# Seven half-size products in place of eight for the q and k of six sequences, in an attention and feed-forward kernel

## The chip, the cores and the metric

The kernel runs on one core of one Trainium2 chip. The metric is the device time of one execution in microseconds (us). The engines are PE (TensorE, matrix products), DVE (VectorE), ACT (ScalarE), POOL (GpSimd) and SP, whose instructions here are DMA issues. Each engine works its own instructions in order, and waits for others by semaphores.

## What is computed

Eight sequences of 512 rows and 256 columns are normalised and go through two branches whose outputs are multiplied: a causal attention with a window of 250 positions, 16 heads of 16 columns and rotated q and k ("rope"), and a three-layer feed-forward part whose weights are +1 or -1.

```python
xn = _layernorm(x)
proj = xn @ in_proj_w.T                      # 256 -> 3 * 256: q, k, v
q, k = _apply_rope(q, k)                     # ya = xa*cos - xb*sin, yb = xa*sin + xb*cos
mask = (delta >= 0) & (delta < CONTEXT)      # delta = row - column, CONTEXT = 250
scores = where(mask, q @ k.T * D ** -0.5, lowest)
s = (softmax(scores) @ v) @ out_proj_w.T
h = s0 * conn_dense(k0, concatenate([xn, -xn])); h = relu(h) * 2
h = s1 * conn_dense(k1, h);                      h = relu(h) * 2
g = silu(s2 * conn_dense(k2, h))
x = x + s * g
```

## The kernel before

**Layout.** Everything is held transposed: 128 partitions carry columns (or heads), the free axis the 512 positions T of a sequence. The 256 columns of q are sorted so that part "a" (128) holds the first member of each rotated pair and part "b" the second; the same for k.

**Order.** Instructions are issued from a list of pieces, each with a time written by hand, in units of which a sequence takes 42 (`SEQ`); a piece can return further pieces with delays, which `run` (L234) keeps in a heap and issues when the running cost has passed their time. The order in which they are issued is the order on every engine. While sequence b goes through its 16 feed-forward layers' tiles and its 6 attention steps, the inputs of sequence b + 1 are prepared: in units of b, its moments at 9, normalisation at 18.4, k at 23.0 and 24.5, q at 26.0 and 27.5.

**Normalisation.** `norm_turned` (L300) subtracts and multiplies the transposed x (`xT`) by the moments spread over partitions (`of_all`, L309, on DVE), and splits the result into a 16-bit high part (ACT) and a low part (DVE) for the feed-forward layers. `of_all` has one buffer (tag "mb", shared with part b of the rope products).

**Feed-forward.** `layer` (L511 products, L520 low part `h2l` on DVE, L522 high part `h2h` on ACT) is what PE does most of the time. Products of high parts ("h high") and of low parts ("h low") of a tile can be issued apart. `z` is the last layer (L562), whose silu needs an exponential, a sum, a reciprocal (L633, DVE, in halves) and a product with the gate (L635, POOL).

**q and k.** `project` (L371) makes 128 columns by 512 positions in one PSUM bank from two products (L381: two chunks of 128 columns of x). Each product is one instruction in the program and two records in the profile. DVE multiplies the bank by cosine and sine (`rope_sb`, L397: two operations of 128x512, reading PSUM), POOL adds and subtracts the four (`rotate`, L418), ACT rounds the result into a high half (`split_hi`, L434, tag "hi": one buffer for k and q), DVE makes the low half as the difference (`split_lo`, L441), and each half is written to DRAM at once by two DMAs of 512 KB on SP (`to_dram`, L427: `dk`, `dq`). `stack` (L450) loads them back, 16 partition rows of several heads at a time, as the operands of the scores (`k<-dk`, `q<-dq`, 256 KB each).

**Attention.** A step is six banks of scores (`sc`, L746), exponentials (L771, ACT), masks of the window (L791, L798, POOL) and products with v (`po`, L828) of the step before. `keep` (L840) moves a group's result to `V` and its row sums to `S` (three buffers; L846 and L847 on DVE, L852 and L853 on ACT); `gather` (L918, `dsums<-S`), `pack` (L926, `sums<-dsums`), `invert` (L932 to L938) and `unpack` (L945) turn the sums into reciprocals via DRAM, and `divide` spreads them (`R`, L951) and multiplies `V` (L952, POOL). `project_o` (`att_ps`, L962) and L984, L991 finish the output with the residual `xr` (loaded by L545). The last sequence has outputs of 256 positions, with a copy of PSUM on ACT (L974) and sums on POOL (L975, L977).

PSUM has eight banks: seven rotate over all uses that ask for `bank(...)`, one is kept for `po`.

Of the kernel before, what the change touches and what calls it, by code (L numbers as in the profile page):

```python
# [11 lines left out]
F32 = mybir.dt.float32  # L12
# [22 lines left out]
def tile_attention_times_gated_ffn(  # L35
# [62 lines left out]
    work = ctx.enter_context(tc.tile_pool(name="work", bufs=2))  # L98
    small = ctx.enter_context(tc.tile_pool(name="small", bufs=4))
    hpool = ctx.enter_context(tc.tile_pool(name="hpool", bufs=1))  # L100
    probs = ctx.enter_context(tc.tile_pool(name="probs", bufs=8))
    dram = ctx.enter_context(tc.tile_pool(name="dram", bufs=2, space=bass.MemoryType.DRAM))
    PSUM = bass.MemoryType.PSUM
    ps_o = ctx.enter_context(tc.tile_pool(name="ps_o", bufs=1, space=PSUM))
# [2 lines left out]
    def bank(name):  # L107
        return ps_b.tile([P, T], F32, tag="b", name=name)
# [56 lines left out]
    def weights(w, p, c, cols):  # L165
        if p == "l":
            return w[:, c, cols]
        return w[:, c].bitcast(F16).rearrange("p (f two) -> p f two", two=2)[:, cols, 1]

    rows = const.tile([P, T], F32, name="rows")  # L170
    nc.vector.memset(rows, 1.0)
# [119 lines left out]
    def lay_over(b):  # L291

        st = states[b]
        of_all = st["of_all"] = turned.tile(
            [P, 2, T], F32, tag="mb", name=f"of_all_{b}", bufs=1
        )
        d = st["moments"].rearrange("(i t) p -> i (t p)", i=2)
        nc.sync.dma_start(of_all, d.partition_broadcast(P))

    def norm_turned(b, c):  # L300

        st = states[b]
        if c == 0:
            st["xT"] = raw_xT.pop(b)
            for p, dt in (("h", F16), ("l", F32R)):
                st["x" + p] = one.tile([P, EC, T], dt, tag="x" + p, name=f"x{p}_{b}")
        xT = st["xT"][:, c]
        for i, op in ((1, ALU.subtract), (0, ALU.mult)):
            nc.vector.tensor_tensor(xT, xT, st["of_all"][:, i], op)  # L309
        hi, lo = (st["x" + p][:, c] for p in "hl")  # L310

        def low():
            nc.vector.scalar_tensor_tensor(lo, xT, sgnx, hi, ALU.mult, ALU.subtract)

        return [(3.2, lambda: nc.scalar.mul(hi, xT, sgnx)), (3.8, low)]

    def norm(b, t):
        mv, xn = states[b]["mv"], xs[b, t]
# [52 lines left out]
    def project(b, what, part, half=None):  # L371

        st = states[b]
        col = E * "qk".index(what) + P * "ab".index(part)
        if half == 1:
            ps = st.pop(part)
        else:
            ps = st[part] = bank(f"{what}{part}_ps_{b}")
        for cols in [slice(0, T)] if half is None else [ts(half, T // 2)]:
            for c in range(EC):  # L380
                nc.tensor.matmul(  # L381
                    ps[:, cols], wqkv_sb[:, c, ds(col, P)], st["xT"][:, c, cols],
                    start=(c == 0), stop=(c == EC - 1),
                )
        if half == 0:
            return

        m = turned.tile(
            [P, 2, T], F32, tag=f"m{part}", name=f"m_{what}{part}_{b}",
            bufs=2 if part == "a" else 1,  # L390
        )
        st[what, part] = m

        hi_after, lo_after = (4.0, 5.1) if b else (5.0, 6.2) if what == "k" else (4.6, 5.4)

        def times(i):
            nc.vector.tensor_tensor(  # L397
                m[:, i], ps, rope_sb[:, i if part == "a" else 1 - i], ALU.mult
            )

        def both():
            times(0)
            times(1)
            if part == "b":
                return [
                    (1.4, lambda: rotate(b, what)),
                    (hi_after, lambda: split_hi(b, what)),
                    (lo_after, lambda: split_lo(b, what)),
                ]


        return [(1.5 if b == 0 and what + part == "qb" else 0.0, both)]

    def rotate(b, what):
        st = states[b]
        m, n = st[what, "a"], st.pop((what, "b"))
        for i, op in enumerate((ALU.subtract, ALU.add)):
            nc.gpsimd.tensor_tensor(m[:, i], m[:, i], n[:, i], op)  # L418
# [34 lines left out]
    def prepare(b, plain=False):  # L453

        if b == 0 or plain:
            at = dict(stats=-40, norm=-38, x=-36, k=0, q=3, v=9.2)
            dp, dv = 1.5, 1.5
        else:

            at = dict(load=9, stats=9, down=10.5, over=12, norm=18.4, k=23.0, q=26.0, v=SEQ + 0.6)  # L460
            if b == 1:
                at.update(load=17.15, stats=14, down=16.9, over=17.2, norm=24.8, k=28.1, q=31.6)
            dp, dv = (0.01 if b == 1 else 1.5), 0.85
            at = {n: SEQ * (b - 1) + f for n, f in at.items()}
        out = [(at["stats"], 0, lambda: stats(b))]
        if "over" in at:
            out += [
                (at["load"], 0, lambda: load_xT(b)), (at["down"], 0, lambda: lay_down(b)),
                (at["over"], 0, lambda: lay_over(b)),
                (at["norm"], 0, lambda: norm_turned(b, 0)),  # L470
                (at["norm"] + 1.2, 0, lambda: norm_turned(b, 1)),
            ]
        for t in range(NT):
            if "over" not in at:
                out += [
                    (at["norm"] + t, 0, lambda t=t: norm(b, t)),
                    (at["x"] + t, 0.25, lambda t=t: turn_x(b, t, plain)),
                ]
            out.append((at["v"] + dv * t, 0.87, lambda t=t: project_v(b, t)))
        for what in "kq":  # L480
            for n, part in enumerate("ab"):
                if b == 0 and what == "k" and not plain:

                    out += [
                        (-34.3 if n == 0 else -32.95, 0.87, lambda p=part: project(b, "k", p, 0)),
                        (at["k"] + dp * n, 0.87, lambda p=part: project(b, "k", p, 1)),
                    ]
                else:
                    out.append((
                        at[what] + dp * n, 1.75, lambda w=what, p=part: project(b, w, p),  # L490
                    ))
        return out
# [37 lines left out]
    def beside(b, u, tag):  # L530

        st = states[b]
        if b + 1 == B and u % 2:
            return st[tag][:, T // 2 :]
        if b + 1 == B and u == 2 and tag == "xr":

            st[tag] = turned.tile([P, 2, T], F32, tag="mb", name=f"xr_{b}_{u}", bufs=1)[:, 0]
        else:
            st[tag] = work.tile([P, T], F32, tag=tag, name=f"{tag}_{b}_{u}", bufs=1)
        return st[tag][:, : T // 2] if b + 1 == B else st[tag]  # L540

    def residual(b, u):
# [296 lines left out]
    def keep(b, g, po):  # L839

        st = states[b]
        odd = g % 2
        S = st["S", g] = outs.tile([P, T], F32, tag="S", name=f"S_{b}_{g}", bufs=3)
        if odd:
            V = st["V", g // 2]
            nc.vector.scalar_tensor_tensor(V, po, second_half, V, ALU.mult, ALU.add)  # L846
            nc.vector.tensor_copy(S, po)  # L847
        else:
            V = st["V", g // 2] = outs.tile(
                [P, T], F32, tag=f"V{g // 2}", name=f"V_{b}_{g}", bufs=2  # L850
            )
            nc.scalar.mul(V, po, first_half)  # L852
            nc.scalar.copy(S, po)  # L853

# [92 lines left out]
    def divide(b, pair):  # L947
        st = states[b]
        V = st["V", pair]
        R = outs.tile([P, T], F32, tag="S", name=f"R_{b}_{pair}", bufs=3)  # L950
        nc.vector.stream_shuffle(R, rows, [D * (n // D) for n in range(32)])  # L951
        return [(0.5, lambda: nc.gpsimd.tensor_tensor(V, V, R, ALU.mult))]  # L952

# [51 lines left out]
    def divisions(b, pairs=(0, 1)):  # L1005
        out = []
        for pair in pairs:
            if b + 1 < B:
                first = SEQ * b + (30.0 if b else 38.4) if pair == 0 else SEQ * (b + 1) + 3.0
            else:  # L1010
                first = SEQ * b + (22.5 if pair == 0 else 33.4)
            pieces = (gather, pack, invert, unpack, divide)
            very_last = b + 1 == B and pair == 1
            for f, at in zip(
                pieces,
                (0.0, 2.0, 4.4, 6.4, 9.0) if very_last
                else (0.0, 2.4, 5.2, 7.6, 15.0 if pair and b + 2 < B else 10.6),
            ):
                out.append((first + at, 0, lambda p=pair, f=f: f(b, p)))
        return out  # L1020
# [17 lines left out]
    def swap():  # L1038
# [5 lines left out]
        (-34.6, 0, signs), (-40.5, 0, lambda: warm(9)), (-34.7, 0, lambda: warm(0)),  # L1044
        (-31.0, 0, lambda: enough(0)),
        (-32.7, 0, lambda: first_parts(2, 3)),
        (19.2, 0, make_w2), (22.5, 0, swap), (SEQ * (B - 1) + 47.6, 0, add_up),
        (SEQ * (B - 1) + 44.0, 0, hint),
    ]
    for c in range(EC):  # L1050
# [153 lines left out]
```

## Time and profile before

Three runs took 599.13, 599.91 and 601.34 us (median 599.91). The profiled execution took 598.2 us, of which 596.5 lie between its first and last instruction; the TensorE clock granted was 0.999 of full speed.

| what | us |
|---|---|
| median of the runs | 599.91 |
| profiled execution | 598.2 |
| its span | 596.5 |
| one sequence in the steady part | 72.05 |
| PE busy in each of the stretches 96:168, 168:240, 240:312, 312:384 | 72.00 |
| DVE, ACT, POOL busy there, mean of one stretch | 41.23, 36.43, 32.82 |
| one product of 128x512 for k or q (2 records) | 0.86 |
| rope multiply, one of 128x512 (L397) | 0.68 |
| low half of q, L441, mean of 8 | 2.09 |
| low half of k, L441, mean of 8 | 1.25 |
| reciprocal of 128x256, mean of 28 | 1.74 |

How to read the views: a timeline row has start and duration in us, engine, line, operation, the tile written, the tiles read, the shapes and a count of instructions; in brackets stand the idle time before it and what ended it. A row of the chain of waits has start, duration, engine, tile, line and count. In the table of stretches the four busy times stand in order PE, PEld (weight loads), DVE, ACT, POOL, with the number of instructions in brackets.

### The profile page before, as it was taken

What the parts mean: (1) busy time and instruction counts of PE and PEld (TensorE: products, weight loads), DVE (VectorE), ACT (ScalarE), POOL (GpSimd) and SP (SyncE); (2) the same over time, 40 slices, a digit from 0 to 9 for tenths busy, and PEclk for the clock granted to TensorE, in tenths of its full rate; (3) what the DMA queues carried; (4) which work ended last, traced back from release to release, by engine and by line L of the source; (5) the groups of instructions that cost most, each with busy time, mean ns of one, the idle gap of its engine ahead of it and who ended that gap; (6) DMA issues with size and microseconds to landing.
All of it is one profiled execution on the core that took longest, in us unless ns stands there. A gap on an engine that the chain in (4) does not pass through costs nothing.

```text
span 596.5 us, 10410 instructions
## 1 busy us (share of the span) xinstructions
PE 584.8 (98%) x3788; PEld 364.7 (61%) x3788; DVE 333.7 (56%) x578; ACT 303.0 (51%) x571; POOL 269.9 (45%) x474
## 2 busy tenths in 40 slices
PE   7999999999999999999999999999999999999996
PEld 6655565655655556555566556665566555657785
DVE  6936335666346754478436684366744666427256
ACT  4747564545464545536454465544644645465422
POOL 2736533436334552445444355333652437435513
PEclk9999999999999999999999999999999999999999
DMA  9764844337432474415654075441673335441111
GB/s 277 283 234 143 294 152 127 108 141 250 146 117 98 170 240 133 147 65 223 208 165 154 2 293 189 130 142 65 238 228 113 107 135 208 158 143 43 35 28 53
DMA packets 50086, 92.24 MB, mean 155 GB/s; under 512 B 10992, under 2 KB 18672, under 8 KB 50032
## 3 DMA queue, kind: packets, MB, share of 16 engines
q1 hardware_dynamic: 47600, 89.31, 44.1%
q10 hardware_dynamic: 2432, 2.23, 1.2%
q8 instruction: 31, 0.51, 0.3%
q14 instruction: 23, 0.19, 0.1%
HBM read 53.22 MB, written 38.30 MB: 153 GB/s over the span
## 4 chain that ended last, share of the span: by engine, by line
PE 88%; DVE 3%; DMA 3%; ACT 2%; SPq 1%; POOL 1%; issue 1%; DVEq 0%; POOLq 0%; ACTq 0%
PE h_ps L511 44%; PE po L828 11%; PE z_ps L562 9%; PE sc L746 7%; PE v_ps L361 4%; PE att_ps L962 4%; PE ka_ps L381 2%; PE qb_ps L381 2%; PE qa_ps L381 2%; PE kb_ps L381 2%; DMA of_all<-d 1%; DMA dq<-m_qa 1%; PE warm L232 1%; SPq L450 1%; DMA dk<-kh 1%
## 5 line engine op out<-in xcount | busy, mean ns | idle before, releaser
L771 ACT ACTIVATE p<-sc 128x512 f32<-128x512 f32 (+2 forms) x288 | 150.2, 607 | 57.6 <-PE sc L746 57.4
L791 POOL TENSOR_SCALAR_AFFINE_SELECT p<-p 128x256 f32<-128x256 f32 (+1 forms) x224 | 104.8, 479 | 123.1 <-ACT p L771 105.4
L511 PE MATMUL h_ps<-h1l,w_sb 128*128 128x512 f32 (+1 forms) x576 | 145.3, 394 | 0.0
L511 PE MATMUL h_ps<-h1h,w_sb 128*128 128x512 f16 (+1 forms) x576 | 123.1, 356 | 0.0
L511 PEld LDWEIGHTS h_ps<-h1l,w_sb 128*128 128x128 f32 x576 | 100.4, 188 | 27.4 <-issue 5.7
L511 PEld LDWEIGHTS <-w_sb 128*128 128x128 f16 x704 | 61.3, 98 | 86.3 <-issue 41.5
L522 ACT ACTIVATE h2h<-h_ps 128x512 f16<-128x512 f32 (+1 forms) x72 | 39.6, 550 | 133.1 <-PE h_ps L511 133.1
L520 DVE SCALAR_TENSOR_TENSOR h2l<-h_ps,h2h 128x512 fp32r<-128x512 f32 (+1 forms) x72 | 44.8, 622 | 93.9 <-ACT h2h L522 93.4
L828 PE MATMUL po<-p,v_pad 128*32 128x378 f32 (+4 forms) x1152 | 71.5, 380 | 0.0
L520 DVE SCALAR_TENSOR_TENSOR h1l<-h_ps,h1h 128x512 fp32r<-128x512 f32 x64 | 43.2, 688 | 45.3 <-ACT h1h L522 45.1
L798 POOL TENSOR_SCALAR_AFFINE_SELECT p<-p 128x256 f32<-128x256 f32 x144 | 57.5, 399 | 0.3 <-POOL p L791 0.3
L746 PEld LDWEIGHTS sc<-q,k 64*128 64x128 f32 x576 | 41.9, 186 | 25.0 <-issue 15.1
L633 DVE RECIPROCAL den<-den 128x256 f32<-128x256 f32 (+1 forms) x32 | 52.4, 1641 | 3.7 <-ACT den L628 3.7
L746 PE MATMUL sc<-q,k 64*128 64x378 f32 (+4 forms) x576 | 52.2, 310 | 2.2 <-ACT p L771 1.2
L522 ACT ACTIVATE h1h<-h_ps 128x512 f16<-128x512 f32 x64 | 37.6, 603 | 30.0 <-PE h_ps L511 30.0
L511 PE MATMUL h_ps<-xl,w_sb 128*128 128x512 f32 x128 | 52.3, 489 | 0.0
L952 POOL TENSOR_TENSOR V<-V,R 128x512 f32<-128x512 f32 x16 | 21.2, 1327 | 52.4 <-DVE R L951 52.4
L828 PEld LDWEIGHTS po<-p,v_pad 128*32 128x32 f32 x1152 | 30.7, 109 | 21.2 <-issue 12.0
L991 POOL TENSOR_TENSOR gate<-gate,xr 128x512 f32<-128x512 f32 (+1 forms) x15 | 18.6, 1242 | 47.6 <-DVE gate L984 26.6
L418 POOL TENSOR_TENSOR m_qa<-m_qa,m_qb 128x512 f32<-128x512 f32 x16 | 21.1, 1343 | 38.5 <-DVE m_qb L397 38.5
L511 PE MATMUL h_ps<-xh,w_sb 128*128 128x512 f16 x128 | 38.5, 383 | 0.0
L562 PE MATMUL z_ps<-h2l,w_sb 128*128 128x512 f32 (+1 forms) x144 | 35.6, 389 | 0.0
(102 smaller groups left out, 656.9 us busy)
## 6 DMA issues: line engine op xcount, KB each, us to landing
k<-dk SPq DMA_DIRECT2D x64, 256.0 KB
q<-dq SPq DMA_DIRECT2D x64, 256.0 KB
dk<-kh SPq DMA_DIRECT2D x16, 512.0 KB
dk<-m_ka SPq DMA_DIRECT2D x16, 512.0 KB
dq<-qh SPq DMA_DIRECT2D x16, 512.0 KB
dq<-m_qa SPq DMA_DIRECT2D x16, 512.0 KB
x<-in_x_dram SPq DMA_DIRECT2D x30, 128.0 KB
xT<-in_x_t_dram SPq DMA_DIRECT2D x7, 512.0 KB
```

What stands on the lines that cost most here:

```text
L361: nc.tensor.matmul(v.rearrange("p n s d -> p (n s d)"), st["xT"][:, c, ts(t, P)], wqkv_sb[:, c, 2 * E :], start=(c == 0), stop=(c == EC - 1),)
L381: nc.tensor.matmul(ps[:, cols], wqkv_sb[:, c, ds(col, P)], st["xT"][:, c, cols], start=(c == 0), stop=(c == EC - 1),)
L511: nc.tensor.matmul(ph, weights(w, p, c, ts(f, P)), st[src + p][:, c, cols], start=(k == 0), stop=(k == n - 1),)
L520: nc.vector.scalar_tensor_tensor(lo, ph, 0.0, hi, ALU.max, ALU.subtract)
L522: high = lambda: nc.scalar.activation(hi, ph, AF.Relu)
L562: nc.tensor.matmul(pz, weights(w2, p, c, ts(f, P)), st["h2" + p][:, c, cols], start=(c == 0 and p == "h"), stop=(c == NF1 - 1 and p == "l"),)
L633: nc.vector.reciprocal(part, part)
L746: nc.tensor.matmul(sc[r + (4 if y else 2 * pair)][:, ds(at, n)], st["k", g, pair][row, ts(j, P)], st["q", g, pair][row, ds(j * P + first, n)],
L771: nc.scalar.activation(p, s_, AF.Exp, scale=D ** -0.5)
L791: nc.gpsimd.affine_select(out=block, in_=block, compare_op=ALU.is_ge, fill=0.0, base=0, pattern=[[0, heads], [1, P]], channel_multiplier=-1,)
L798: nc.gpsimd.affine_select(out=block, in_=block, compare_op=ALU.is_ge, fill=0.0, base=-1, pattern=[[0, heads], [-1, beyond]], channel_multi ...
L828: nc.tensor.matmul(po[32 * r : 32 * r + 32, ds(j * P + first, n)], v_columns(j, g, r), place(tiles_, r, y, off, n), start=(j == 0), stop=( ...
```

## The change

For sequences three to eight (b from 2 to 7), q and k are made by another scheme. A projection of 256 columns into 2 x 128 of q (or k), over 512 positions, is read as a product of a 2 x 2 block matrix of weights with a 2 x 2 block matrix of x (chunks of 128 columns by halves of 256 positions): eight products of 128x128 by 128x256. The new code makes it from seven, with four sums of weight blocks (`w_sums`, made once on POOL for k and q together) and four sums of x blocks (`sum_x`, POOL, 128x256, after `norm_turned` of each chunk, in the buffer of tag "hi").

`project_seven` issues them in two phases into two banks: four products in phase 0, one for each half of each bank; then ACT copies the left half of each bank into SBUF and DVE adds the right half (`u`, and `y` in the tile of part b); three products in phase 1 add to what the banks hold (the left half of both banks and the right half of the second one). Then `quarters` make the four results in SBUF: one copy on ACT, three adds on DVE. The rope multiplies are eight operations of 128x512 in total for k and q, as before, but read SBUF and write in place. `rotate`, `split_hi` and `split_lo` are unchanged; their delays are longer. The pieces stand at 23.0, 24.7, 24.71 and 26.4 units in place of 23.0, 24.5, 26.0 and 27.5.

To make room: `probs` has 7 buffers in place of 8, `S` two in place of three, `R` takes the buffer of tag "hi", `den` moves to the pool `outs`, and the tiles of tag "mb" have two buffers. The last piece of `divisions` for the second pair stands at 14.0 in place of 15.0. Sequences one and two are projected as before.

```diff
-    probs = ctx.enter_context(tc.tile_pool(name="probs", bufs=8))
+    probs = ctx.enter_context(tc.tile_pool(name="probs", bufs=7))
...
+    w_sums = const.tile([P, 4, 2, P], F32, name="w_sums")
+
+    def of_w(c, half):
+        return wqkv_sb[:, c, : 2 * E].rearrange("p (w a f) -> p w a f", w=2, a=2)[:, :, half]
+
+    def sum_weights():
+        s1, s2, s3, s4 = (w_sums[:, i] for i in range(4))
+        sub = lambda out, a, b: nc.gpsimd.tensor_tensor(out, a, b, ALU.subtract)
+        nc.gpsimd.tensor_tensor(s1, of_w(0, 1), of_w(1, 1), ALU.add)
+        sub(s2, s1, of_w(0, 0))
+        sub(s3, of_w(0, 0), of_w(0, 1))
+        sub(s4, of_w(1, 0), s2)
...
         of_all = st["of_all"] = turned.tile(
-            [P, 2, T], F32, tag="mb", name=f"of_all_{b}", bufs=1
+            [P, 2, T], F32, tag="mb", name=f"of_all_{b}", bufs=2
...
+        if b > 1:
+            sum_x(b, c)
...
+    def sum_x(b, c):
+
+        st = states[b]
+        if c == 0:
+            st["x sums"] = turned.tile([P, 4, T // 2], F32, tag="hi", name=f"xs_{b}")
+        t1, t2, t3, t4 = (st["x sums"][:, i] for i in range(4))
+        x11, x12 = (st["xT"][:, 0, ts(k, T // 2)] for k in range(2))
+        x21, x22 = (st["xT"][:, 1, ts(k, T // 2)] for k in range(2))
+        sub = lambda out, a, b: nc.gpsimd.tensor_tensor(out, a, b, ALU.subtract)
+        if c == 0:
+            sub(t1, x12, x11)
+        else:
+            sub(t2, x22, t1)
+            sub(t4, x21, t2)
+            sub(t3, x22, x12)
...
-            bufs=2 if part == "a" else 1,
+            bufs=2,
...
+    def project_seven(b, what, phase):
+
+        st = states[b]
+        H2 = T // 2
+        n = "kq".index(what)
+        w = "qk".index(what)
+        s1, s2, s3, s4 = (w_sums[:, i, w] for i in range(4))
+        w11, w12, w22 = (of_w(c, half)[:, w] for c, half in ((0, 0), (1, 0), (1, 1)))
+        t1, t2, t3, t4 = (st["x sums"][:, i] for i in range(4))
+        x11, x21, x22 = (
+            st["xT"][:, c, ts(half, H2)] for c, half in ((0, 0), (1, 0), (1, 1))
+        )
+
+        def products(which, start):
+            for bank_, half, a, b_ in which:
+                nc.tensor.matmul(
+                    st["seven"][bank_][:, ts(half, H2)], a, b_,
+                    start=start and half == 0, stop=True, skip_group_check=True,
+                )
+
+        if phase == 0:
+            st["seven"] = [bank(f"{what}{i}_ps_{b}") for i in range(2)]
+            products(((0, 0, w11, x11), (0, 1, s2, t2), (1, 0, s3, t3), (1, 1, s1, t1)), True)
+            u = st["u"] = outs.tile([P, H2], F32, tag="u", name=f"u_{what}_{b}")
+            first, second = st["seven"]
+            for part in "ab":
+                st[what, part] = turned.tile(
+                    [P, 2, T], F32, tag=f"m{part}", name=f"m_{what}{part}_{b}", bufs=2
+                )
+            y = st[what, "b"][:, 1, H2:]
+
+            def sums():
+                for out, ps in ((u, first), (y, second)):
+                    nc.scalar.copy(out, ps[:, :H2])
+                    nc.vector.tensor_tensor(out, out, ps[:, H2:], ALU.add)
+
+            return [(0.0, sums)]
+
+        products(((0, 0, w12, x21), (1, 0, w22, t4), (1, 1, s4, x22)), False)
+        first, second = st["seven"]
+        u, m, o = st["u"], st[what, "a"], st[what, "b"]
+
+        def quarters():
+            nc.scalar.copy(m[:, 1, :H2], first[:, :H2])
+            nc.vector.tensor_tensor(m[:, 1, H2:], second[:, H2:], u, ALU.add)
+            nc.vector.tensor_tensor(o[:, 1, :H2], second[:, :H2], u, ALU.add)
+            nc.vector.tensor_tensor(o[:, 1, H2:], o[:, 1, H2:], u, ALU.add)
+            return [(0.3 if n else 2.0, times)]
+
+        def times():
+            for t, order in ((m, (0, 1)), (o, (1, 0))):
+                for i, r in enumerate(order):
+                    nc.vector.tensor_tensor(t[:, i], t[:, 1], rope_sb[:, r], ALU.mult)
+            hi_after = 6.0 if n else 6.9
+            return [
+                (1.4, lambda: rotate(b, what)),
+                (hi_after, lambda: split_hi(b, what)),
+                (hi_after + 1.1, lambda: split_lo(b, what)),
+            ]
+
+        return [(0.0, quarters)]
...
+        if b > 1 and not plain:
+            for (what, phase), at_ in zip(
+                itertools.product("kq", range(2)), (23.0, 24.7, 24.71, 26.4)
+            ):
+                out.append((
+                    SEQ * (b - 1) + at_, 1.29 if phase else 1.72,
+                    lambda w=what, i=phase: project_seven(b, w, i),
+                ))
+            return out
...
-            st[tag] = work.tile([P, T], F32, tag=tag, name=f"{tag}_{b}_{u}", bufs=1)
+            pool = outs if tag == "den" else work
+            st[tag] = pool.tile([P, T], F32, tag=tag, name=f"{tag}_{b}_{u}", bufs=1)
...
-        S = st["S", g] = outs.tile([P, T], F32, tag="S", name=f"S_{b}_{g}", bufs=3)
+        S = st["S", g] = outs.tile([P, T], F32, tag="S", name=f"S_{b}_{g}", bufs=2)
...
-        R = outs.tile([P, T], F32, tag="S", name=f"R_{b}_{pair}", bufs=3)
+        R = turned.tile([P, 2, T], F32, tag="hi", name=f"R_{b}_{pair}")[:, 0]
...
-                else (0.0, 2.4, 5.2, 7.6, 15.0 if pair and b + 2 < B else 10.6),
+                else (0.0, 2.4, 5.2, 7.6, 14.0 if pair and b + 2 < B else 10.6),
...
+        (27.0, 0, sum_weights),
```

## The prediction

> **What bounds the kernel now.** I read the page's busy times first, then its chain of work that ended last.
>
> ```profile
> PE 584.8 (98%) x3788; PEld 364.7 (61%) x3788; DVE 333.7 (56%) x578; ACT 303.0 (51%) x571; POOL 269.9 (45%) x474
> PE 88%; DVE 3%; DMA 3%; ACT 2%; SPq 1%; POOL 1%; issue 1%; DVEq 0%; POOLq 0%; ACTq 0%
> ```
>
> TensorE (PE) is busy for 98% of 596.5 us, so products taken off it are worth their full time as long as nothing else becomes late. Whether something does is decided where sequence 4 is projected while sequence 3 is computed; the other sequences repeat this every 72 us. There the chain of waits runs on PE alone, without a gap:
>
> ```profile
> 258.70 1.83 PE h_ps L511 x8
> 260.54 1.72 PE ka_ps L381 x4
> ...
> 271.15 1.72 PE qb_ps L381 x4
> 272.87 1.00 PE sc L746 x12
> ...
> 291.47 3.59 PE h_ps L511 x16
> 295.06 0.99 PE sc L746 x11
> ```
>
> The scores at 295.06 are the first that read the new q and k. They come through DRAM, so I read VectorE (DVE) and the queue SP in the timeline:
>
> ```profile
> 270.52 1.22 DVE L441 TENSOR_TENSOR m_ka<-m_ka,kh 128x1024 fp32r<-128x1024 f32 x1
> 273.00 1.75 DVE L633 RECIPROCAL den<-den 128x256 f32<-128x256 f32 x1 [0.49 <-ACT den L628]
> 275.81 1.74 DVE L633 RECIPROCAL den<-den 128x256 f32<-128x256 f32 x1
> 279.01 2.29 DVE L441 TENSOR_TENSOR m_qa<-m_qa,qh 128x1024 fp32r<-128x1024 f32 x1 [1.46 <-ACT qh L434]
> 271.76 1.39 SPq L427 DMA_DIRECT2D dk<-m_ka  x2
> 281.32 1.02 SPq L427 DMA_DIRECT2D dq<-m_qa  x2
> 286.86 0.32 SPq L926 DMA_DIRECT2D sums<-dsums  x1
> 289.19 0.42 SPq L450 DMA_DIRECT2D q<-dq  x1
> ```
>
> The low half of k (L441) is done at 271.74, before two reciprocals, and its 1 MB leaves over an idle queue; that of q ends at 281.30. SP then goes in order through dsums, sums and the loads of k and q. The trace's DMA records let the last q load land at 293.84, and the second score pair needs it at 295.34: the path has **1.5 us of slack** (1.2 to 1.9 over the sequences). In the second sequence it has none: the waits list PE's scores 1.0 us for q<-dq at 79.0.
>
> **The change, part by part.**
>
> *PE.* Each tensor had four products of 512 columns, 2 x 1.72 = 3.44 us. Seven of 256 take their place. The nearest row is the same size of product for v:
>
> ```profile
> 299.13 0.86 PE v_ps L361 x4
> ```
>
> Four records of 256 columns take 0.86 us where four of 512 take 1.72 (ka above), exactly half; the weight load (189 ns, mean of the v group) stays below the 215 ns of one record. A product is two records, so seven cost 7 x 0.43 = 3.01 us. Gain 0.43 us a tensor, 0.86 a sequence, six sequences: **-5.2 us**. Bounds: nothing, if the loads came out of cover, and -5.2 as by the row; I take the row.
>
> A rule in the Trainium skill, TensorE: Matmul & The Clock Gate, section "Back-to-back issue gap", speaks against halved products: each warm matmul pays about 2.5 ns beside its columns. A product here takes the time of four passes of that kind, so by the rule 24 more passes a sequence cost 0.06 us, and the gain would be about 4.8 instead of 5.2 us; the v row, where halves make a whole, shows no such share.
>
> *Additions on PE's own path.* Phase 1 adds into the banks whose upper and lower halves DVE has combined in place, so it waits for ScalarE (ACT) copies and DVE adds. A PE stretch of h (1.73 to 1.88 us) lies between the phases. Copy .37 + add .41 (the 128x256 rows of L974 and L984), twice and overlapped, leaves about 0.9 us of it. Cost nothing; without the h stretch it would be 0.9 us a phase. The four sums of x on GpSimd (POOL) are 0.73 us each (L635, 128x256); the last two are due at 261.0 to 261.4 and ready by my order at 258.3 to 261.5: bounds 0 and 0.1, I take 0. The sums of weights, once: four POOL operations, 2.9 us, at about 50 us. They push the rotation of the second sequence's q by 1.1 and its way to the scores by about 0.4, where PE waits already: **+0.4 us**.
>
> *DVE.* Added are five adds a tensor, 10 x 0.41 = 4.1 us a sequence. The rope multiplies become 8 of SBUF by SBUF at 0.69 instead of 8 from PSUM at 0.68. These reach another regime: the trace shows that a DVE operation on two SBUF inputs and a POOL operation shut each other out.
>
> ```profile
> 254.21 1.76 DVE L309 TENSOR_TENSOR xT<-xT,of_all 128x512 f32<-128x512 f32 x1 [0.16 <-DMA of_all<-d]
> 275.38 2.52 POOL L418 TENSOR_TENSOR m_qa<-m_qa,m_qb 128x512 f32<-128x512 f32 x2 [6.23 <-DVE m_qb L397]
> 280.17 1.39 POOL L791 TENSOR_SCALAR_AFFINE_SELECT p<-p 128x256 f32<-128x256 f32 x1
> ```
>
> The first takes 1.76 against 0.69 for its like (it began beside POOL's V at 254.13, 1.29 long), and the low half of q 2.29 against 1.22; the select of 0.40 takes 1.39 beside it. Multiplies from PSUM (274.67, under the rotation) keep 1.22 a pair. So eight more operations and four adds can now wait for a whole rotation (1.27) each time.
>
> *Order.* This is the main step. Compared instruction by instruction, the order on DVE is now: sums and quarters of k, four multiplies of k, quarters and multiplies of q, h2l, two reciprocals, and only then the low half of k, then that of q. I ran this by hand with the durations above. With collisions: multiplies of q end 275.8, rotation 278.2, h2l 276.4, reciprocals 279.7, low k 281.1 (before 271.74). Next late is the high half of q on ACT: it shares k's one "hi" buffer, so it runs at 281.1 to 282.2 (before 277.93 to 278.98), and the low half of q ends at 283.7 (before 281.30). Without any collision low k ends 279.5 and low q 281.9.
>
> *SP and the transfers.* Behind low k wait dk's 1 MB, then xr 0.25, dq high 1 and dq low 1 MB, 3.25 MB in a row, and dsums, sums and the loads queue behind these. Before, dk was away by 276.4 and q's path was alone. The window from 270 to 296 us moves 397 to 410 GB/s when full, 0.39 MB/us with gaps: 8.3 us. From 280 (no collisions, after the issue) that ends at 288.3 and the last write lands about 288.9; from 282 (collisions) at 290.3 to 291. Before, sums were issued at 286.86, when dsums were there, and the last q landed 6.98 later. So q lands at 295.9 or about 297.95, **2.06 or 4.1 us later**. Since the rows pay the whole of the other instruction when they collide, but not each operation meets one, I take two thirds of the way: 3.4 us. The lower end for the order alone, without a backlog of transfers, is the 0.6 that low q moves (281.9 against 281.30).
>
> *The masks and a shared bank.* POOL's masks now stand behind q's rotation and the gate product behind them; exponentials wait behind the copies of k and q on ACT. The sixth score pair of a step is put in the bank of its first, so PE waits there for the first exponential: by the hand order 285.0 against 284.2, 0.8 us; bounds 0.35 and 0.8. The 0.86 that PE gained just before covers it: both vanish in the wait for q.
>
> *Sum.* PE reaches the next scores at -0.86 + 0.8, about where it was, and q is 3.4 late against 1.5 of slack: 1.9 us lost in each of six sequences, 11.4, and 0.4: profiled run 598.2 + 11.8 = 610.0. This run stands 1.7 under the median of 599.91, so **611.7 us**. The ends: 2.06 gives 599.9 + 3.4 + 0.4 = 603.7; 4.1 gives 615.9; slack 1.2 in place of 1.5 another 1.8.
>
> **Rivals.** *Full gain (faster).* If low k is issued early enough that q's path stays within its slack, and the bank is free, 599.9 - 5.2 + 0.4 = 595.1. It decides as long as q lands less than 0.6 us later (1.5 - 0.86). For it: DVE has 6.8 us of waits between 262.29 and 281.30 before, which 4.1 us of adds could fill. Against it: 1 MB more must leave behind the reciprocals on queues that ran at 0.4 MB/us.
>
> *The gain is eaten by the sixth score pair.* q is in time, PE waits 0.8 us in the shared bank: 599.9 - 5.2 + 6 x 0.8 + 0.4 = 599.9. For it: the shared bank is in the order, in all six; against it: the same as above, for it also needs q.
>
> *A later wait beside q's.* S has two buffers in place of three, and dsums are issued behind dq low, so ACT's copy of the third S (286.78 before) waits for dsums to land (290 to 291) and evictions of h stand behind it. It costs where h then finds no free bank, at 1.5 us a sequence beyond q's wait: 611.7 + 9 = 620.7. Against it: PE would wait for q anyway, and the banks give a few us.
>
> **How the numbers follow.** Forecast 611.7 us at 0.61, own range 603.7 to 617.7 (both ends of q's lateness, the upper with slack 1.2); full gain 0.17; shared bank 0.14; later wait 0.08. What a measurement can tell from no change is about 0.5%, 596.9 to 602.9. So faster 0.17, same 0.14, slower 0.69. The range from 597 to 619 takes in the forecast and the shared bank and leaves out the full gain and most of the later wait.
>
> **What would show it.** Right: PE scores waiting for q<-dq some 2 us at each new sequence, PE's busy time 5 us lower, the low half of k after two reciprocals near 281, transfers without a gap behind it. Products of 0.43 us in pairs of records show the first term; DVE rows of SBUF multiplies above 1 us show the collisions. Wrong: no wait for q<-dq, or the reciprocals coming later than I ordered them, or the low half of q ending before 281.5; then one of the first two rivals holds. Waits of ACT's S copy for dsums, and of PE for h banks, would show the third.

## The result, and the profile after

The changed kernel takes **630.27 us** (median of 6 runs, 626.83 to 635.33) against 599.52 us (6 runs, 597.72 to 601.34): a ratio of 1.052 with a 95% interval of 1.048 to 1.056. It is slower by 30.75 us. The profiled execution took 632.67 us, 34.5 more than that of before; its span is 630.9.

The page's busy times, its shares of the chain, and the granted clock in 40 slices:

```profile
PE 598.9 (95%) x3860; PEld 387.4 (61%) x3860; DVE 364.7 (58%) x638; ACT 314.9 (50%) x607; POOL 306.4 (49%) x502
PE 63%; DVE 13%; DMA 9%; SPq 4%; POOL 4%; ACT 3%; issue 3%; POOLq 0%; ACTq 0%; DVEq 0%
PEclk9998989999899998999989999899999999999999
```

TensorE's part of the chain fell from 88% to 63%; VectorE, the transfers and the queue SP took its place. The third row is the surprise: six of the slices have the digit 8, one for each stretch at half clock told of below. TensorE's busy time *rose* by 14.1 us although it has less to do, in part because some of that work ran at half clock.

The waits of TensorE (in total, times, the longest). Before, all waits for q together were 1.0 us.

```profile
PE sc L850 <- DMA q<-dq: 14.6, 9, 2.6
PE sc L850 <- ACT p L875: 4.4, 8, 2.2
...
PE po L932 <- POOL p L902: 1.9, 1, 1.9
```

The same place as in the prediction, sequence 4 projected while sequence 3 is computed. First the chain (start, duration, what):

```profile
279.97 1.73 PE k_ps L461 x8
281.70 1.87 PE h_ps L614 x8
283.57 1.29 PE k_ps L461 x6
284.86 1.74 PE q_ps L461 x8
...
295.90 3.27 DVE den L737 x2
299.17 1.09 DVE m_ka L535
300.32 1.06 ACT qh L528
301.40 1.79 DVE m_qa L535
...
307.18 3.54 DMA dsums<-S
310.78 0.32 SPq L1030
...
312.58 5.15 DMA q<-dq
317.97 0.88 PE sc L850 x5
```

It leaves TensorE at q's first phase and comes back at 317.97, by way of both reciprocals, the two low halves (L535), the transfers queued on SP, and q. The sizes of single steps stand in the timeline of VectorE:

```profile
285.57 0.42 DVE L492 TENSOR_TENSOR m_kb<-m_kb,u_k 128x256 f32<-128x256 f32 x1
...
290.69 0.85 DVE L492 TENSOR_TENSOR m_qb<-m_qb,u_q 128x256 f32<-128x256 f32 x1
291.46 2.50 DVE L498 TENSOR_TENSOR m_qa<-m_qa,rope_sb 128x512 f32<-128x512 f32 x2
293.88 1.41 DVE L498 TENSOR_TENSOR m_qb<-m_qb,rope_sb 128x512 f32<-128x512 f32 x2
```

The add on two SBUF inputs takes 0.85 us for q where the same add for k took 0.42, and a pair of multiplies 2.50 where the next pair takes 1.41. Both met POOL's rotation of k (289.46 to 292.69). The adds that read PSUM kept 0.42 and 0.41 us beside that rotation (at 290.02 and 290.36).

To compare the kernels I count from the start of k's first product (260.54 before, 279.97 after):

| us after k's first product | before | after | later by |
|---|---|---|---|
| low half of k ends | 11.2 | 20.3 | 9.1 |
| low half of q ends | 20.8 | 23.2 | 2.5 |
| sums issued (dsums have landed) | 26.3 | 30.8 | 4.5 |
| last q has landed | 33.3 | 37.8 | 4.5 |
| the score pair that needs it | 34.8 | 38.0 | 3.2 |

**An account of the profiled run.** The start of a sequence's v products marks its period. Before, the six later periods were 72.05 us each. After, the first is 72.36 against 65.04, and the others are 77.68, 76.67, 77.03, 76.55, 75.18 and 74.48. The first four of those hold one stretch at half clock each, the first period two. Such a stretch costs 1.71 us (below). Without it the six are longer by 3.1 us on average, 18.5 in all; the stretches add 6 x 1.71 = 10.2; the rest of the first period is 3.9; the start varies from run to run and was 1.9 later. Together 34.5.

### The profile page after: what moved, and what is told of

It reads as the page before. It is cut to its first block, busy times and chain, and to the rows that moved or that the text cites. A ratio compares the mean times of both kernels' runs of the same rounds, so it can differ in the third digit from the quotient of the medians.

```text
span 630.9 us, 10724 instructions
## 1 busy us (share of the span) xinstructions
PE 598.9 (95%) x3860; PEld 387.4 (61%) x3860; DVE 364.7 (58%) x638; ACT 314.9 (50%) x607; POOL 306.4 (49%) x502
## 4 chain that ended last, share of the span: by engine, by line
PE 63%; DVE 13%; DMA 9%; SPq 4%; POOL 4%; ACT 3%; issue 3%; POOLq 0%; ACTq 0%; DVEq 0%
PE h_ps L614 28%; PE po L932 9%; PE z_ps L666 9%; PE sc L850 5%; DMA q<-dq 5%; PE v_ps L393 4%; DMA dsums<-S 3%; PE k_ps L461 3%; DVE m_qa L498 2%; SPq L521 2%; DVE den L737 2%; PE q_ps L461 1%; DVE m_qa L535 1%; SPq L544 1%; DVE m_kb L498 1%
## 5 line engine op out<-in xcount | busy, mean ns | idle before, releaser
L895 POOL TENSOR_SCALAR_AFFINE_SELECT p<-p 128x256 f32<-128x256 f32 (+1 forms) x224 | 103.1, 471 | 105.5 <-ACT p L875 83.3
L614 PE MATMUL h_ps<-h1l,w_sb 128*128 128x512 f32 (+1 forms) x576 | 143.4, 391 | 0.0
L932 PE MATMUL po<-p,v_pad 128*32 128x378 f32 (+4 forms) x1152 | 78.3, 406 | 1.9 <-POOL p L902 1.9
L850 PE MATMUL sc<-q,k 64*128 64x378 f32 (+4 forms) x576 | 59.7, 318 | 20.8 <-DMA q<-dq 14.6
L850 PEld LDWEIGHTS sc<-q,k 64*128 64x128 f32 x576 | 45.7, 189 | 45.2 <-issue 19.5
L902 POOL TENSOR_SCALAR_AFFINE_SELECT p<-p 128x256 f32<-128x256 f32 x144 | 63.1, 438 | 0.3 <-POOL p L895 0.3
L932 PEld LDWEIGHTS po<-p,v_pad 128*32 128x32 f32 x1152 | 33.3, 116 | 26.4 <-issue 15.5
L512 POOL TENSOR_TENSOR m_ka<-m_ka,m_kb 128x512 f32<-128x512 f32 x16 | 24.4, 1545 | 49.1 <-DVE m_kb L498 39.5
```

The source lines that it names most:

```text
L614: nc.tensor.matmul(ph, weights(w, p, c, ts(f, P)), st[src + p][:, c, cols], start=(k == 0), stop=(k == n - 1),)
L850: nc.tensor.matmul(sc[r + (4 if y else 2 * pair)][:, ds(at, n)], st["k", g, pair][row, ts(j, P)], st["q", g, pair][row, ds(j * P + first, n)],
L895: nc.gpsimd.affine_select(out=block, in_=block, compare_op=ALU.is_ge, fill=0.0, base=0, pattern=[[0, heads], [1, P]], channel_multiplier=-1,)
L902: nc.gpsimd.affine_select(out=block, in_=block, compare_op=ALU.is_ge, fill=0.0, base=-1, pattern=[[0, heads], [-1, beyond]], channel_multi ...
L932: nc.tensor.matmul(po[32 * r : 32 * r + 32, ds(j * P + first, n)], v_columns(j, g, r), place(tiles_, r, y, off, n), start=(j == 0), stop=( ...
```

## Half clock after a wait

The windows of the sequence above and of one later, cut where the clock can change (stretch, its length; busy time of PE, PEld, DVE, ACT, POOL; granted clock; DMA share; GB/s):

```profile
312.68:316.10 3.42, 2.62 (x13) 1.74 (x11) 2.73 (x7) 1.70 (x4) 0.86 (x2) 1.00 0.89 282
316.10:319.51 3.41, 1.54 (x20) 1.06 (x24) 0.00 (x0) 0.38 (x1) 1.00 (x1) 1.00 0.46 167
319.51:322.92 3.41, 3.41 (x39) 1.85 (x32) 1.05 (x3) 1.08 (x2) 0.51 (x2) 0.50 0.48 131
...
469.70:473.11 3.41, 1.78 (x28) 1.30 (x32) 0.00 (x0) 0.69 (x2) 1.10 (x1) 1.00 0.57 196
473.11:476.52 3.41, 3.41 (x39) 2.27 (x32) 1.17 (x3) 2.28 (x5) 0.52 (x2) 1.00 0.52 142
```

Every stretch at half clock in these runs starts on a grid of 3.41 us and lasts one or two of its steps; the last one of a run is cut short by its end. The wait up to 317.97 leaves TensorE busy for 1.54 of 3.41 us, and the next step runs at 0.50; the wait up to 471.33 (2.00 us) leaves 1.78 busy, and the next step keeps 1.00. So a wait of about 2 us costs itself, and 1.71 more or nothing by where it falls on the grid. The kernel before has no such stretch until its end.

The Trainium skill (TensorE: Matmul & The Clock Gate, section "What's actually happening") gives a free-running window of 3413 ns, which is the grid seen here. It puts the throttle behind an idle window, and the section "HAM oscillation — how this bites in real kernels" words the rule as no gaps above about 3.4 us; here a window that was busy for 45% was enough, after a wait of 2.56 us, and the measurement decides.

## The experiments

Each ratio is against the kernel before in the same set of runs, with its 95% interval. The first four were planned against the theory "q is late because of the order on VectorE and the transfers behind it".

**Old products, low half of k late.** The kernel before, with its low half of k moved behind the reciprocals:

```diff
-hi_after, lo_after = (4.0, 5.1) if b else ...
+hi_after, lo_after = ((7.5, 8.6) if what == "k" and b > 1 else (4.0, 5.1)) if b else ...
```

> The kernel before, with eight products and PSUM multiplies as they were, and only the order of the change: the low half of k behind both reciprocals on DVE, its high half behind the sum on ACT, for sequences three to eight. Theory (order, eight more additions and collisions each hold a part): low q ends at most 1 us later and the writes of k pile up before those of q, q lands 1 to 2 us later, of which 1.5 us are slack: 599 to 605 us. Rival (the order alone makes the loss): 615 us or more.

607.59 us (605.60 to 609.73), ratio 1.0151 (1.0106 to 1.0196), between the two expectations. The period is 73.3 us: the sixth score pair of the step costs 0.35 more, and the second score pair of the new sequence comes 0.87 later. The order alone makes the sums 2.7 us later, not the 4.5 of the change, and the waits for q stay below 1 us:

```profile
PE sc L746 <- DMA q<-dq: 2.8, 5, 0.7
```

No half clock follows. The order is a true part of the loss, and not the whole.

**Low half of k early.** The changed kernel, with the copy and the low half of k ahead of the exponentials and reciprocals:

```diff
-hi_after = 6.0 if n else 6.9
+hi_after = 6.0 if n else 4.0
```

> The changed kernel, with the high half of k ahead of the sum and the exponentials on ACT, and the low half of k ahead of the two reciprocals on DVE, its writes with it. Theory (the low half of k behind the reciprocals makes q and the writes late): low k ends 3 us earlier, low q 1.5 us earlier, the wait shrinks from 2.9 to 1 us or less and the half clock goes in part: 609 to 621 us. Rival (q's loads are set by dsums and by what DVE has to do in all): within 4 us of 630.

622.42 us (620.97 to 624.20), ratio 1.0379 (1.0334 to 1.0423), 1.4 us beyond the theory's range. In the profiled run the periods are 75.03 us, with a stretch at half clock in each. The wait for q is nearly gone and the sixth score pair is back at 0.99 us, but the exponentials now stand behind the copy of k, and a product of h waits for the bank that they free:

```profile
PE h_ps L614 <- ACT p L875: 12.4, 6, 2.1
PE sc L850 <- DMA q<-dq: 2.4, 2, 1.4
```

The wait for q went for two reasons. Counted from k's first product, in the same sequence, the low half of k ends 2.7 us earlier than in the change, that of q 1.3, and the sums are issued 2.6 earlier: so 2.6 of the 4.5 us by which q is late come from the place of the low half of k, which agrees with the run before. And TensorE itself, with its new wait of 2.1 us and the half clock behind it, comes to these scores 3.0 us later than in the kernel before, and finds q there.

**The loads first.** The step that issues sums and waits for dsums is put behind the first loads of k and q:

```diff
-(0.0, 2.4, 5.2, 7.6, ...)
+(0.0, 2.4 if pair or b == 0 or b + 1 == B else 3.2, 5.2, 7.6, ...)
```

> The changed kernel, with the load of the row sums (sums<-dsums) issued behind the first loads of k and q in place of ahead of them, in sequences two to seven. Theory (the q loads stand in SP's order behind a load that waits for dsums to land, some 4 us after the last write of q was issued): q lands 2 to 4 us earlier, the wait of the scores and the half clock behind it go, 604 to 615 us. Rival (3.25 MB of writes and 1 MB of loads need their time whatever the order): q lands less than 1 us earlier, 624 us or more.

628.79 us (625.83 to 629.41), ratio 1.0477 (1.0429 to 1.0524): a miss, the rival's range holds. The last load of q is issued 1.1 us earlier in the same sequence (0.9 on average), and the wait for q halves. The scores now wait for as long for a bank that `h2l` has yet to read. The instruction ahead of `h2l` on VectorE reads `sums`, which now come later: it waits up to 9.4 us, against 4.8 in the change.

```profile
PE sc L850 <- DMA q<-dq: 7.4, 5, 2.2
PE sc L850 <- DVE h2l L623: 7.3, 12, 1.4
DVE sums L1036 <- DMA sums<-dsums: 47.0, 6, 9.4
```

**The sums of weights later**, one sequence on:

```diff
-(27.0, 0, sum_weights)
+(SEQ + 2.0, 0, sum_weights)
```

> The changed kernel, with the four sums of weights made 20 us later, after the masks of the first step of the second sequence, and nothing else moved. Theory (the sums stand between a step's masks, so products with v wait 1.9 us, the scores at 83 us wait 1.3 us longer than before, and each of the two waits is followed by some 3.4 us at half the granted clock, 1.7 us each): 6 to 7 us less, 623 to 625 us. Rival (the prediction's term of 0.4 us is right and the first sequences are slow for another reason): 629 to 631 us.

632.38 us (626.74 to 634.59), ratio 1.0565 (1.0510 to 1.0621): a miss by the median. What the edit was for did happen: the first period fell from 72.36 to 70.67 us, and the wait of the products with v is gone. In the change that wait comes from POOL, where the sums stand amid one step's masks:

```profile
51.24 0.41 POOL L895 TENSOR_SCALAR_AFFINE_SELECT p<-p 128x256 f32<-128x256 f32 x1
51.62 0.73 POOL L178 TENSOR_TENSOR w_sums<-wqkv_sb 128x256 f32<-128x256 f32 x1
...
53.80 0.73 POOL L177 TENSOR_TENSOR w_sums<-wqkv_sb,w_sums 128x256 f32<-128x256 f32 x1
54.48 0.41 POOL L895 TENSOR_SCALAR_AFFINE_SELECT p<-p 128x256 f32<-128x256 f32 x1
```

```profile
55.30 0.83 PE L932 MATMUL po<-p,v_pad 128*32 128x378 f32 x4 [1.90 <-POOL p L902]
```

The second fence is the timeline of TensorE there. With the sums moved, the scores of the second sequence still wait, 0.86 us for q and 0.72 for exponentials. The gain is hidden by the half clock, whose share differs from run to run. Taking the time that each run's mean clock lost (span times 0.999 less the clock) off each run leaves 616.8 to 620.0 us here and 618.3 to 622.6 for the change. That is 2 to 3 us better, a reading that rests on this correction.

**Seven eighths of the products and nothing else.** The kernel before; for sequences three to eight the last product of k and of q, on the second chunk of x, covers the first 256 positions alone, so an eighth of the projection is left out.

```diff
+part_ = slice(0, T // 2) if b > 1 and half is None and part == "b" and c else cols
-ps[:, cols], wqkv_sb[:, c, ds(col, P)], st["xT"][:, c, cols],
+ps[:, part_], wqkv_sb[:, c, ds(col, P)], st["xT"][:, c, part_],
```

> The kernel before, with one eighth of the q and k projections of sequences three to eight left out (the second chunk of x for the last 256 positions of part b), and everything behind it as it was. Theory (a half product of 0.43 us less per tensor is worth its full time when nothing behind it changes, and q's 1.5 us of slack covers that PE is 0.86 us earlier): 5.2 us less than before, 593 to 595 us beside 598.6. Rival (halved products pay a fixed part, or q becomes late at once): 596 us or more.

594.72 us (594.08 to 595.17), ratio 0.9910 (0.9879 to 0.9940). Its chain has 1.29 us where four records of whole products take 1.72, and the period is 71.19, shorter by exactly the 0.86 of the prediction:

```profile
264.33 1.29 PE kb_ps L382 x4
```

**The whole change in another order, twice.** Seven products with other due times, so that the multiplies of k follow its quarters sooner (a) or later (b), and with the exponentials, the gate steps, the row sums and the low parts of h shifted to suit. The core of each:

```diff
 # a
-return [(0.3 if n else 2.0, times)]
+return [(0.3 if n else 0.75, times)]
-hi_after = 6.0 if n else 6.9
+hi_after, lo_after = (5.38, 7.19) if n else (6.9, 8.0)
-(23.0, 24.7, 24.71, 26.4)
+(22.23, 24.7, 24.71, 25.94)
-(27.0, 0, sum_weights)
+(46.23, 0, sum_weights)
 # b
-return [(0.3 if n else 2.0, times)]
+return [(0.3 if n else 3.01, times)]
-hi_after = 6.0 if n else 6.9
+hi_after, lo_after = (3.94, 7.1) if n else (2.67, 5.05)
-(23.0, 24.7, 24.71, 26.4)
+(23.0, 23.85, 25.46, 25.87)
-(27.0, 0, sum_weights)
+(42.91, 0, sum_weights)
```

> All of the change, in another order: the sigmoid's sum and reciprocals half a unit earlier, the high and low halves of q 0.6 and 0.1 units nearer their product, k's products 0.8 units earlier and the multiplies of k ahead of the sums of q, the row sums gathered 0.6 units earlier, the sums of weights after the masks. The low half of k stays behind both reciprocals. Theory (the place of the reciprocals and q's way are what cost, the products do gain): q is in time, no half clock, PE keeps some 1 us of waits a sequence (second phase of q, shared score bank): 597 to 602 us. Rival (the additions and collisions on DVE make q late in any order): 610 us or more.

> As gates_early_a, but with the high halves of k and q rounded much earlier on ACT (2.67 and 3.94 units after their multiplies, low halves after 5.05 and 5.04) and k's multiplies late. Theory as there: 597 to 602 us. Rival: 610 us or more. If a is fast and b slow, the place of the roundings on ACT counts too.

612.46 us (611.19 to 616.17), ratio 1.0197 (1.0154 to 1.0241), and 615.39 (611.72 to 616.76), ratio 1.0245 (1.0187 to 1.0303): much of the loss goes, and none of the gain comes. Both lie beyond the theory's range and in the rival's; scores still wait for q, and half clock still follows some of the waits. In both, the second phase of q waits for the sums that VectorE makes in its banks. The waits of TensorE in a:

```profile
PE sc L850 <- DMA q<-dq: 5.7, 5, 2.1
PE q_ps L461 <- DVE u_q L480: 4.3, 6, 0.7
```

0.72 us a sequence is nearly the 0.86 that the products save. In b a sequence without a wait for q takes 72.80 us: the 0.86 saved is more than paid back by this wait, 0.62 more in the sixth score pair, and about 0.3 elsewhere.

**That wait taken away.** Version b with the sums of q issued 0.41 units later, and so after the products of the second phase. They then read banks that hold all seven products, so that q is not what the change computes.

```diff
-return [(0.0, sums)]
+return [(0.41 if n else 0.0, sums)]
```

(Four due times beside it are shifted: the multiplies of q, the last piece, the residual, and the step of sums.)

> gates_early_b, with the sums of q issued 0.41 units after their products, q's multiplies 0.46 after its quarters, q's second phase 0.2 units earlier, the residual's load 1.7 units later, and sums<-dsums 0.84 units later (behind the loads of k and q). Theory (the wait of q's second phase, 0.72 us in gates_early_a and b, comes from k's multiplies standing ahead of the sums of q): that wait goes, a period of 71.6 to 72.1 us against 72.8, 599 to 607 us by the number of half clocks. Rival (DVE has no room): 610 us or more.

600.43 us (598.45 to 604.41), ratio 1.0035 (1.0007 to 1.0064), no half clock. Periods run from 71.83 to 72.8. The wait at q's second phase is gone, but b's waits for q fell from 6.0 to 2.2 us in the same step, so the 15 us between b and this run aren't the price of that one wait. What is left is the shared bank: the sixth score pair holds TensorE from 284.40 to 286.01, 1.61 us in place of 0.99, and so takes back 0.62 of the 0.86. Its last products wait for the first exponential:

```profile
285.59 0.49 PE L850 MATMUL sc<-q,k 64*128 64x244 f32 x3 [0.25 <-ACT p L875]
```

Even an order that has almost no waits left only comes back to the time of before.

**A pause on purpose.** To price a wait without the change, the kernel before gets, in each of six sequences, a tiny product, two (short) or five (long) POOL operations on a scratch tile, and a tiny product that waits for them.

```diff
+if b and u == 0 and how == "later":
+    nc.tensor.matmul(pz[:, :1], idle, idle[:, :1], start=True, stop=True)
+    for _ in range(5):
+        nc.gpsimd.tensor_tensor(idle, idle, idle, ALU.mult)
+    nc.tensor.matmul(pz[:, :1], idle, idle[:, :1], start=True, stop=True)
```

> The kernel before, with one pause of PE in each of sequences two to seven, ahead of the first product of the last layer (z): a tiny product, two POOL operations of 128x128 on a scratch tile, a tiny product that reads it. The result is the same. Theory (a wait costs its length, and half a clock window of 3.41 us more, 1.7 us, only where about half of one such window is idle): a wait of about 1.0 us a sequence, no half clock, 6 to 8 us more than before. Rival (any wait lowers the clock): 14 us or more, with half clock behind each.

> As pause_short, with five POOL operations in place of two. Theory: a wait of about 2.3 us a sequence, 14 us, and behind several of the six a window of 3.41 us at half clock, 1.7 us each: 17 to 25 us more than before in all, the spread between runs being multiples of 1.7 us. Rival (the half clock in the changed kernel came from its other waits or from the halved products, not from the wait): 13 to 15 us more and no half clock.

Short: 609.56 us (608.47 to 610.70), ratio 1.0191 (1.0171 to 1.0212). That is 11.2 us where 6 to 8 were expected: a period grows by 1.52, of which 1.02 are the wait and 0.5 the tiny products themselves, which I had not priced; the start of the profiled run was 1.4 later. No half clock follows any of the six waits. Long: 622.61 us (619.94 to 627.70), ratio 1.0417 (1.0356 to 1.0478). That is 24.2 us, inside the theory's 17 to 25 and beyond the rival's 15; the wait is 2.45 us each time, and half clock follows two of six in the profiled run. Its windows behind one wait that was followed by half clock and one that wasn't:

```profile
162.70:166.11 3.41, 0.99 (x7) 0.80 (x5) 0.69 (x1) 0.97 (x2) 1.99 (x5) 1.00 0.06 13
166.11:169.52 3.41, 3.38 (x9) 1.46 (x10) 0.00 (x0) 0.00 (x0) 0.00 (x0) 0.50 0.02 5
...
241.20:244.61 3.41, 1.82 (x11) 0.99 (x11) 0.00 (x0) 0.00 (x0) 1.30 (x4) 1.00 0.00 0
244.61:248.03 3.42, 3.42 (x26) 2.46 (x28) 0.75 (x1) 0.72 (x2) 0.00 (x0) 1.00 0.00 0
```

The same wait of 2.45 us leaves 0.99 busy in the first case and 1.82 in the second. Of the other four, the one that was followed by half clock left 1.39, and the three that weren't left 1.92, 2.01 and 2.10. This shows the half clock as an effect of the wait and its place on the grid, apart from anything that the change does.

## Why the prediction was partly right

**Right.** The direction and the place: scores wait for q at each new sequence, because the low half of k stands behind two reciprocals (it ends 20.3 us after k's first product; by hand 20.6) and that of q follows (2.5 later; by hand 2.4). The gain on TensorE: 1.73 us for eight records and 1.29 for six, and the seven-eighths kernel is 5.4 us faster where 5.2 were forecast. The shared bank: the sixth score pair costs 1.05 us more, 0.8 by hand. Collisions on VectorE showed, though on fewer operations than the prediction allowed for: it counted four of the ten adds of a sequence as able to collide, and only two read SBUF alone (L492, one a tensor).

**A sign that failed.** TensorE's busy time should have been 5 us lower and was 14.1 higher. The six stretches at half clock explain at most 10.2 of that; the rest stays open.

**Mis-sized: q's lateness.** The prediction said "Since the rows pay the whole of the other instruction when they collide, but not each operation meets one, I take two thirds of the way: 3.4 us". It was 4.5, above even the upper end of 4.1. The hand order with collisions was exact to 0.1 us for the low half of q; the backlog was not: from the low half of q to dsums landing takes 7.6 us in place of 5.6, which is 2.0 more, where the upper end held 1.7. From the sums on, q takes the 6.95 us that it took before (6.98). The slack was counted to q's landing as 1.5 us; 0.24 of it goes from landing to the product. So 4.5 less 1.3 is 3.2 us lost in this sequence, 3.1 on average, in place of 1.9: about 7 us of the miss.

**Missing: the clock.** The sum has no term for what a wait does to the work behind it. The prediction looked only for how long TensorE waits. The profiled run lost 10.2 us to six stretches at half clock. By the mean clocks of all six runs (0.973 to 0.991) they lost 5 to 16.5, with a median of 8.2.

**Mis-sized: the sums of weights.** "+0.4 us" priced the push on q's rotation. The four operations stand amid one step's masks, so the products with v wait 1.9 us, of the 3.9 us that the first period lost beside half clock. Another 1.3 (2.24 less 0.97) are the later wait, under "The rivals", and 0.7 were not traced.

Together: 18.5 a run from q, 3.9 from the first period and about 8.2 from the clock are 30.6, against 30.75 measured. The first two come from the profiled run and the third is a median of six, so that they meet this closely is in part luck.

**The rivals.** The full gain and the shared bank as the end of it fall with the wait for q. (For the full gain the prediction counted 6.8 us of waits on VectorE between 262.29 and 281.30. VectorE is busy for 13.23 of these 19.01 us, so 5.8 are free, which still holds the 4.1 of the adds.) The shared bank is real all the same: where q is in time, in the run with that wait taken away, it costs 0.62 us a sequence. The later wait did come, on ScalarE:

```profile
ACT S L957 <- DMA dsums<-S: 30.1, 7, 4.6
```

No product of h waits for a bank in the list of TensorE's waits, but in the second sequence the wait reached TensorE by way of the scores. ScalarE's copy of the third `S` stands for 4.31 us, the exponentials stand behind it, and the scores wait 2.24 us for a bank that these free. The kernel before has no wait of ScalarE for `dsums`, and its TensorE waited 0.97 us there, for q (last row):

```profile
84.85 0.59 ACT L957 COPY S<-po 128x512 f32<-128x512 f32 x1 [4.31 <-DMA dsums<-S]
85.98 1.44 PE L850 MATMUL sc<-q,k 64*128 64x378 f32 x8 [2.24 <-ACT p L875]
79.03 0.89 PE L746 MATMUL sc<-q,k 64*128 64x378 f32 x8 [0.97 <-DMA q<-dq]
```

The step of 3.41 us with this wait is busy for 1.34 us, and one of the six stretches at half clock follows. In the later sequences the scores wait for exponentials 0.3 us on average; there the wait for q is the one that ends last. No run gives the third buffer of `S` back, so that its lack is the cause is argued from the order and not shown.

**Open.** Of the 4.5 us the order alone explains 2.7 (old products, low half late). How the other 1.8 divide between the added operations and their collisions wasn't tried apart, nor were the fewer and shared buffers that the change needs (`probs`, `S`, the tag "hi"). Nor is it shown that no order keeps the gain: of the versions that compute the same result with seven products, the best took 612.46 us.

## What to carry to other kernels

Products taken off a busy TensorE are worth their full time, here 0.86 us a sequence, only if nothing is added to the path that feeds it; ten additions on VectorE, four sums on POOL and one instruction moved behind two reciprocals took that back and 3.1 us more. Where an instruction that releases a transfer moves, count the bytes that then leave in a row, and follow the one queue to the transfer that TensorE waits for. Where a forecast ends in a wait of TensorE, price it twice: the wait itself, and half clock behind it, 1.71 us here, if it leaves less than about 1.6 us of a 3.41 us step busy; up to 2.0 us it came in some cases.

## What was not expected of the hardware

Half clock after short waits. In the traces of these runs, past the first 10 us, every step of 3.41 us at full clock with TensorE busy for less than 1.57 us was followed by a step at half clock, and none busy for more than 2.00 was. In between the busy time of the profile doesn't decide: steps with 1.64 and, in the run with the loads first, 1.73 and 2.00 us were followed by half clock, those with 1.57 (also there), 1.78 and 1.82 were not. The case of 2.00:

```profile
236.46:239.87 3.41, 2.00 (x13) 1.17 (x11) 1.22 (x5) 1.57 (x3) 0.00 (x0) 1.00 0.78 242
239.87:243.29 3.42, 3.25 (x28) 1.69 (x32) 1.31 (x3) 0.57 (x2) 1.28 (x1) 0.50 0.03 4
```

It makes a time scatter: the change's runs spread over 8.5 us, those of the kernel before over 3.6. With the time that each run's mean clock lost taken off, the change's spread is 4.3.
